# Layer 3's mean square taken from the layer norm's moments, and ScalarE for the last step of two quarters' norms

## The chip, the cores and the metric

The kernel runs on one core of one Trainium2 chip. The metric is device time in microseconds (us) of one execution; a kernel is run several times and the median counts. PE is the matrix engine (TensorE), DVE is VectorE, ACT is ScalarE, POOL is GpSimd and SP is the engine that issues most DMAs. [...]

## What is computed

The reference has four layers on an activation of 4 sequences of 1024 tokens with 128 features, in float32. Each layer is an attention-like mixer and a feed-forward block, each followed by a residual add and a layer norm without weights. Layer 2 has causal attention with 16 heads; the feed-forward blocks of layers 1, 2 and 3 route each token to some of 16, 8 and 32 experts. The change is in the mixer of layer 3:

```
def _layernorm(x, axis=-1, eps=1e-05):
    m = jnp.mean(x, axis=axis, keepdims=True)
    v = jnp.var(x, axis=axis, keepdims=True)
    return (x - m) / jnp.sqrt(v + eps)
...
    rms = jnp.linalg.norm(query, axis=-1, keepdims=True) * e ** (-0.5)
    x = query / (rms + EPS)
    u = jax.nn.silu(jnp.einsum('nbe,fe->nbf', x, u_w) + u_b)
    v = jax.nn.silu(jnp.einsum('nbe,fe->nbf', x, v_w) + v_b)
...
    y = _toeplitz_mix(vh, pos, zero, neg)
...
    out = u * y
    return jnp.einsum('nbf,ef->nbe', out, o_w) + o_b + query
```

`query` is the layer norm's result, with one row per token. Its root mean square `rms` can be had in two ways: from the normalised row itself, or from the norm's moments, since a row with variance v that was divided by sqrt(v + eps) has the mean square v / (v + eps).

## The kernel before, in words

**Tiles and parts.** The tokens lie in 32 tiles of 128 tokens by 128 features, in one SBUF tensor `x`. A quarter is 8 tiles: 256 positions of each of the 4 sequences. Layer 3 works on three parts: part a is quarters 0 and 1, part b is quarter 2, part c is quarter 3 (`self.first`, `self.rest`, L110).

**The norm.** `norm` (L185) takes a list of tiles. Per tile it issues `bn_stats` and `bn_aggr` on VectorE (L191, L192), which leave mean and variance in `mv`. Then it makes `rstd`, one over the root of variance plus epsilon, in one of several ways: with `by="act"` a Sqrt on ScalarE (L195) and a reciprocal on VectorE (L196); with `by="dve"` by `rsqrt` (L171), which is an integer guess and three Newton steps, 14 small VectorE operations. Last, one VectorE operation per tile subtracts the mean and multiplies by `rstd` (L205).

**Layer 3's mixer.** `l3_attn(part, exps)` (L1548) goes through the quarters of a part. `exps=True` is for part a, which runs while ScalarE computes the exponentials of layer 2's attention: Sqrt and Silu are avoided there, `by="dve"` is used, and Silu is put together from Tanh and VectorE operations. For a quarter the order is: norm (L1576); for each half of 4 tiles the squares (L1584), their sum per row (L1585), the root (by `rsqrt` at L1590 to L1592, or a Sqrt at L1594), scale and epsilon (L1595), the reciprocal (L1596), the row times this factor into `sq` (L1598), twice `x` plus a bias as the residual (L1600), and four PE transposes with a copy into `xq` (`transposes`, L159; the copy is L167 on ScalarE or L169 on VectorE). Then come the projections u and v with Silu (L1567, or L1570 to L1572), the Toeplitz mix on VectorE (L1626 to L1632), the output projection and residual (L1641), the second norm (L1643) and its transposes (`turned`, L1646).

**What follows it.** `l3_route` (L1650) makes router logits, softmax, the top 4 and, in `positions` (L1231), the place of each row in the lists of the experts (`pos...`, L1272). `spread` (L1309) scatters the rows into a list in DRAM with one indirect DMA on GpSimd per tile and choice (L1297). `l3_shared` (L1671) is the shared expert, whose result is added to `x` (L1687). `l3_experts` (through `small_experts`, L1699) gathers the list in groups of 4 tiles (L1328, issued by SP, which needs all scatters of the part) and works through it: transposes, gate and up, Silu (L1729), product (L1730), transposes, down, and a copy out (L1744 on ScalarE, L1747 on VectorE). `collect` (L1377) gathers each token's expert results with indirect DMAs on GpSimd and adds them to `x` (L1388); `finish` (L1782) and `close` (L1857) norm and store.

**What sets the order.** All of these are generators that issue instructions and then yield a planned cost in us: `yield (7.0,)` after the norm, `yield (4.0,)` after the mean square of a half, `yield (2.3,)` after a transposition, and so on. `mix(main, side, pace)` (L233) advances `side` until its planned cost times `pace` has caught up with what `main` has yielded; with `drain=False` the rest of `side` stays for later. `press` (L1844) advances the side alone until a condition holds. `abreast` (L1816) advances several generators at equal planned times. `served` (L1805) lets other generators go first as soon as their condition holds. An extra order is put on side instructions: each goes behind the latest instruction of the main on its engine (`queued`, L223).

In `all` (L1868), part a's mixer and routing are the side of layer 2's attention for the second half of the positions (`l2_attn(1)`, pace 1), then of layer 2's experts for the parts m and n, which also wait for their own routing; part b's mixer and routing are the side of part a's shared expert and experts (pace 0.75); then b's scatter, with part c's mixer and routing `abreast`, goes ahead of, and beside, part b's experts; part c's scatter and part b's collection go beside part c's experts; `close` of part c ends the kernel. After the last experts a branch on a flag can start a general path, which this data doesn't take.

Of the kernel before, what the change touches and what calls it, by code (L numbers as in the profile page):

```python
# [14 lines left out]
AF = mybir.ActivationFunctionType  # L15
ALU = mybir.AluOpType
AX = mybir.AxisListType
# [3 lines left out]
P = 128  # L21
B, L, D = 4, 1024, 128
# [8 lines left out]
QT = NT // NQT  # L31
# [43 lines left out]
class Kernel:  # L75
# [106 lines left out]
            ts(t, t, -0.5, 1.5, ALU.mult, ALU.add)  # L182
            tt(y, y, t, ALU.mult)

    def norm(self, tiles, by="act"):  # L185

        nc, n = self.nc, len(tiles)
        mv = self.tile(self.small, [P, n, 2], f"mv{n}")
        for t, x in enumerate(tiles):
            st = self.tile(self.small, [P, 6], "bn")  # L190
            nc.vector.bn_stats(st, x)  # L191
            nc.vector.bn_aggr(mv[:, t, :], st)  # L192
        rstd = self.tile(self.small, [P, n], f"rstd{n}")
        if by == "act":
            nc.scalar.activation(rstd, mv[:, :, 1], AF.Sqrt, bias=self.eps)  # L195
            nc.vector.reciprocal(rstd, rstd)  # L196
        else:
            ve = self.tile(self.small, [P, n], f"ve{n}")
            nc.vector.tensor_scalar(ve, mv[:, :, 1], LN_EPS, None, ALU.add)
            if by == "pool":  # L200
                nc.gpsimd.tensor_tensor(rstd, ve, self.mhalf[:, :n], ALU.pow)
            else:
                self.rsqrt(rstd, ve)
        for t, x in enumerate(tiles):
            nc.vector.tensor_scalar(x, x, mv[:, t, 0:1], rstd[:, t : t + 1], ALU.subtract, ALU.mult)  # L205

    def quarter(self, q):

# [1339 lines left out]
    def l3_attn(self, part, exps=False):  # L1548


        nc, tc, x, xT, col = self.nc, self.tc, self.x, self.xT, self.col
        stt = nc.vector.scalar_tensor_tensor
        NC = D13 // P
        with ExitStack() as ctx:
            cp = self.pool(ctx, "l3c" + part.name, right=True)
            vp = self.pool(ctx, "l3v" + part.name, right=True)
            ps = self.side
            wuv = self.load(cp, self.ins["l3_uv"])
            wo = self.load(cp, self.ins["l3_o"])
            if exps:  # L1560
                hb = self.tile(cp, [P, 2 * NC], "hb")
                nc.vector.tensor_scalar(hb, col["l3_b"], 0.5, None, ALU.mult)

            def silu(dst, pz, i):

                if not exps:
                    nc.scalar.activation(dst, pz, AF.Silu, bias=col["l3_b"][:, i : i + 1])  # L1567
                    return
                th = self.tile(vp, [P, BLK], "th", bufs=2)
                nc.scalar.activation(th, pz, AF.Tanh, bias=hb[:, i : i + 1], scale=0.5)  # L1570
                stt(dst, pz, col["l3_b"][:, i : i + 1], th, ALU.add, ALU.mult)
                stt(dst, pz, col["l3_b"][:, i : i + 1], dst, ALU.add, ALU.add)  # L1572

            for q in range(part.q0, part.q0 + part.nq):
                s = slice(q * QT, (q + 1) * QT)
                self.norm(self.quarter(q), by="dve" if exps else "act")  # L1576
                yield (7.0,)
                xq = self.tile(vp, [P, QC], "xq")
                rms = self.tile(self.small, [P, QT], "rms")
                for g in range(2):  # L1580
                    sg = slice(q * QT + g * 4, q * QT + g * 4 + 4)
                    r = rms[:, g * 4 : g * 4 + 4]
                    sq = self.tile(vp, [P, 4, D], "sq")
                    nc.vector.tensor_tensor(sq, x[:, sg, :], x[:, sg, :], ALU.mult)  # L1584
                    nc.vector.tensor_reduce(r, sq, AX.X, ALU.add)  # L1585
                    if exps:

                        ri = self.tile(self.small, [P, 4], "rmsi")
                        v = self.tile(self.small, [P, 4], "rmsv")
                        nc.vector.tensor_scalar(v, r, 1e-30, None, ALU.max)  # L1590
                        self.rsqrt(ri, v)
                        nc.vector.tensor_tensor(r, r, ri, ALU.mult)  # L1592
                    else:
                        nc.scalar.activation(r, r, AF.Sqrt)  # L1594
# [13 lines left out]
                    yield (2.3,)  # L1608
                u = self.tile(vp, [P, NC, B, TQ], "u")
                for c in range(NC):  # L1610
                    v = self.tile(vp, [P, B, TQ], "v")
                    for i, dst in ((1, v), (0, u[:, c])):
                        for g in range(2):
                            pz = self.tile(ps, [P, BLK], "s")
                            self.mm(pz, wuv[:, i, c * P : (c + 1) * P], xq[:, g * BLK : (g + 1) * BLK])
                            silu(dst[:, 2 * g : 2 * g + 2, :].rearrange("p b t -> p (b t)"), pz, i * NC + c)
                            yield (2.3,)

                    cf = col["toep"][:, c * 7 : (c + 1) * 7]
                    for i in range(B):  # L1620
                        y = self.tile(vp, [P, TQ], "y", bufs=1 if exps else 2)
                        for j in range(B):
                            lag = i - j
                            a = lag if lag >= 0 else 3 - lag
                            if j == 0:
                                nc.vector.tensor_scalar(y, v[:, j, :], cf[:, a : a + 1], None, ALU.mult)  # L1626
                            else:
                                stt(y, v[:, j, :], cf[:, a : a + 1], y, ALU.mult, ALU.add)
                        if exps:
                            stt(u[:, c, i, :], u[:, c, i, :], 0.25, y, ALU.mult, ALU.mult)  # L1630
                        else:
# [486 lines left out]
```

## Time and profile before

| | us |
|---|---|
| median of 3 runs | 2064.29 |
| lowest, highest of these | 2057.93, 2067.41 |
| the profiled execution, own time | 2440.36 |
| its span, first to last instruction | 2438.2 |
| PE busy | 1619.9 (66%) |
| VectorE busy | 1303.3 (53%) |
| ScalarE busy | 789.9 (32%) |
| GpSimd busy | 774.0 (32%) |
| mean granted TensorE clock | 0.813 |

The profile is of one execution, which took 18% more than the median of the unprofiled runs. Its times are counted from the first instruction. A row of the timeline names start, duration, engine, operation, output and inputs with their shapes, and in square brackets the engine's idle time before it with what released it ("remote" or "issue" where the profile shows no releaser). A row of a stretch has its limits, its length, then for each engine its busy time and its number of instructions, then the granted clock and the share of the DMA engines. Small operations overlap a little, so the pitch from start to start says more than a single duration.

### The profile page before, as it was taken

Reading aid. Unit: us, or ns where it says so; the run is one execution under the profiler, and the core shown is the slowest. Engines: PE = TensorE matmul, PEld = TensorE weight load, DVE = VectorE, ACT = ScalarE, POOL = GpSimd, SP = SyncE. Lnnn points to the kernel's source line nnn. Section 1 sums busy time; section 2 is a strip of 40 time slices with the busy share of each in tenths; the row PEclk is TensorE's granted clock in tenths of the full one; section 3 lists DMA queues with packets and bytes.
Section 4 is the critical chain, followed back from the end, with each engine's and each line's share of the span. In section 5 each row is a group of like instructions: output and inputs, shape, how many; then the busy total and the mean of one; then the engine's idle time right before and its main releaser. Section 6 shows DMA issues by size and latency. Waiting matters only on the chain. (4 is left out here: it accounts for less than half of the span.)

```text
span 2438.2 us, 27135 instructions
## 1 busy us (share of the span) xinstructions
PE 1619.9 (66%) x9017; PEld 962.6 (39%) x9017; DVE 1303.3 (53%) x3732; ACT 789.9 (32%) x1114; POOL 774.0 (32%) x701
## 2 busy tenths in 40 slices
PE   7535776875661775687968787887853898267080
PEld 3214333753320344545623232345532586154070
DVE  8767795655570564324535665464711378247053
ACT  5511372322230432222336454642211254122030
POOL 5531285145227002224132002002164201736704
PEclk9766787988785888888979898988876998577595
DMA  9930002334101014312120000031141141223132
GB/s 308 288 104 0 13 33 82 117 120 159 60 31 52 14 73 142 100 48 70 44 96 21 1 1 17 2 117 35 42 174 40 44 127 45 71 71 96 51 100 59
DMA packets 215530, 187.10 MB, mean 77 GB/s; under 512 B 16528, under 2 KB 194064, under 8 KB 214864
## 3 DMA queue, kind: packets, MB, share of 16 engines
q1 hardware_dynamic: 194672, 142.29, 18.5%
q0 software_dynamic: 20704, 42.86, 5.7%
q8 instruction: 84, 1.38, 0.2%
q14 instruction: 70, 0.57, 0.1%
HBM read 88.49 MB, written 96.60 MB: 76 GB/s over the span
## 5 line engine op out<-in xcount | busy, mean ns | idle before, releaser
L1051 ACT ACTIVATE pr<-sc 128x1024 f32<-128x1024 f32 x288 | 279.6, 1021 | 326.1 <-PE sc L157 197.7
L157 PE MATMUL gu<-ld,xgT 128*128 x640 | 172.1, 413 | 81.9 <-issue 36.6
L157 PE MATMUL sc<-qm,kT 32*128 32x512 f32 (+3 forms) x1536 | 200.2, 564 | 15.9 <-ACT pr L1051 12.0
L157 PE MATMUL s<-pr,va 128*32 128x512 f32 (+3 forms) x1536 | 177.3, 531 | 46.0 <-issue 27.9
L157 PEld LDWEIGHTS gu<-ld,xgT 128*128 128x128 f32 x640 | 123.6, 204 | 109.5 <-issue 48.0
L157 PE MATMUL gu<-wall,xgT 128*128 x304 | 161.0, 657 | 3.2 <-ACT xgT L167 2.0
L1057 DVE TENSOR_TENSOR pr<-pr,ld 128x512 f32<-128x512 f32 (+1 forms) x160 | 92.5, 581 | 101.3 <-ACT pr L1051 98.8
L169 DVE COPY hT<-tp 128x512 f32<-128x512 f32 x118 | 81.0, 686 | 120.7 <-PE tp L165 50.4
L165 PE MATMUL tp<-ld,hg 128*128 128x128 f32 x624 | 100.6, 285 | 50.4 <-DVE hT L169 35.4
L157 PEld LDWEIGHTS sc<-qm,kT 32*128 32x128 f32 x1536 | 85.5, 200 | 119.5 <-issue 66.6
L165 PE MATMUL tp<-ld,xg 128*128 128x128 f32 x396 | 66.3, 295 | 90.9 <-issue 50.7
L165 PEld LDWEIGHTS tp<-ld,hg 128*128 128x128 f32 x624 | 80.1, 147 | 104.8 <-DVE hT L169 42.2
L167 ACT COPY xgT<-tp 128x512 f32<-128x512 f32 x99 | 58.0, 587 | 195.4 <-PE tp L165 126.9
L1730 DVE TENSOR_TENSOR hg<-sg,gu 128x256 f32<-128x256 f32 x160 | 65.7, 416 | 102.5 <-ACT sg L1729 94.8
L1494 ACT ACTIVATE sg<-gu 128x512 f32<-128x512 f32 x76 | 45.2, 597 | 226.3 <-PE gu L157 115.3
L1297 POOL DMA_INDIRECT l1ra<-x,posl1a x64 | 95.6, 1494 | 60.5 <-DVE posl1a L1272 41.3
L1729 ACT ACTIVATE sg<-gu 128x256 f32<-128x256 f32 x160 | 60.6, 384 | 157.3 <-PE gu L157 85.7
L157 PE MATMUL pu<-xT,ld 128*128 128x512 f32 x104 | 65.0, 719 | 60.1 <-issue 58.5
L1297 POOL DMA_INDIRECT yt<-l1yr,posl1r x64 | 60.7, 948 | 139.2 <-DVE x L1388 78.8
L157 PEld LDWEIGHTS s<-pr,va 128*32 128x32 f32 x1536 | 38.7, 113 | 156.6 <-issue 110.6
L1496 DVE TENSOR_TENSOR hg<-sg,gu 128x512 f32<-128x512 f32 x76 | 51.8, 681 | 87.2 <-ACT sg L1494 43.9
L1297 POOL DMA_INDIRECT l1rr<-x,posl1r x64 | 61.7, 964 | 99.6 <-DVE posl1r L1272 80.4
(443 smaller groups left out, 3551.7 us busy)
## 6 DMA issues: line engine op xcount, KB each, us to landing
wall<-wall SPq DMA_DIRECT2D x16, 768.0 KB
l3ra<-zero SPq DMA_DIRECT2D x1, 6144.0 KB
ld<-in_l_w SPq DMA_DIRECT2D x2, 3072.0 KB
wall<-we SPq DMA_DIRECT2D x24, 256.0 KB
ld<-in_l_w SPq DMA_DIRECT2D x1, 6144.0 KB
l1ra<-zero SPq DMA_DIRECT2D x1, 5120.0 KB
l1rr<-zero SPq DMA_DIRECT2D x1, 5120.0 KB
xg<-l3ra SPq DMA_DIRECT2D x20, 256.0 KB
```

What stands on the lines that cost most here:

```text
L157: return self.nc.tensor.matmul(out, lhsT, rhs, start=start, stop=stop)
L165: nc.tensor.transpose(pt[:, k * P : (k + 1) * P], s, self.ident)
L167: nc.scalar.copy(dst, pt[:, : n * P])
L169: nc.vector.tensor_copy(dst, pt[:, : n * P])
L1051: nc.scalar.activation(pr, sc[h], AF.Exp)
L1057: nc.vector.tensor_tensor(d, d, cst["tril"].unsqueeze(1).unsqueeze(1).to_broadcast([P, 2, n, P]), ALU.mult)
L1297: ins = self.nc.gpsimd.indirect_dma_start(**kw)
L1494: nc.scalar.activation(sg, gu[:, 0, :], AF.Silu)
L1496: nc.vector.tensor_tensor(h, sg, gu[:, 1, :], ALU.mult)
L1729: nc.scalar.activation(sg, pg[:, :, 0, :], AF.Silu)
L1730: nc.vector.tensor_tensor(h[:, 2 * c : 2 * c + 2, :], sg, pg[:, :, 1, :], ALU.mult)
```

## The change

The norm gets an argument `on_act` and returns its moments and `rstd`. With `on_act`, minus mean times `rstd` is computed for all tiles in one VectorE operation (`off`), and the last step of each tile becomes a ScalarE activation, Identity of `rstd` times `x` plus `off`. In `l3_attn` both norms take it where `exps` is false, that is in quarters 2 and 3.

The mean square of all 8 tiles of a quarter comes from the variance in `mv`: its root times `rstd`, plus epsilon, inverted. The squares and their sums over 512 elements go, and the root is taken once for 8 columns in place of twice for 4. The planned costs become 6.0 after the first norm, 2.0 once for the root mean square, none for the halves' 4.0, and 5.0 after the second norm.

```diff
-    def norm(self, tiles, by="act"):
+    def norm(self, tiles, by="act", on_act=False):
...
+        if on_act:
+            off = self.tile(self.small, [P, n], f"off{n}")
+            nc.vector.scalar_tensor_tensor(off, mv[:, :, 0], -1.0, rstd, ALU.mult, ALU.mult)
         for t, x in enumerate(tiles):
-            nc.vector.tensor_scalar(x, x, mv[:, t, 0:1], rstd[:, t : t + 1], ALU.subtract, ALU.mult)
+            if on_act:
+                nc.scalar.activation(x, x, AF.Identity, bias=off[:, t : t + 1], scale=rstd[:, t : t + 1])
+            else:
+                nc.vector.tensor_scalar(x, x, mv[:, t, 0:1], rstd[:, t : t + 1], ALU.subtract, ALU.mult)
+        return mv, rstd
...
-                self.norm(self.quarter(q), by="dve" if exps else "act")
-                yield (7.0,)
+                mv, rstd = self.norm(self.quarter(q), by="dve" if exps else "act", on_act=not exps)
+                yield (6.0,)
...
+                if exps:
+
+                    v = self.tile(self.small, [P, QT], "rmsv")
+                    nc.vector.tensor_scalar(v, mv[:, :, 1], 1e-30, None, ALU.max)
+                    self.rsqrt(rms, v)
+                    nc.vector.tensor_tensor(rms, rms, mv[:, :, 1], ALU.mult)
+                else:
+                    nc.scalar.activation(rms, mv[:, :, 1], AF.Sqrt)
+                nc.vector.tensor_tensor(rms, rms, rstd, ALU.mult)
+                nc.vector.tensor_scalar(rms, rms, 1e-8, None, ALU.add)
+                nc.vector.reciprocal(rms, rms)
+                yield (2.0,)
                 for g in range(2):
...
-                    nc.vector.tensor_tensor(sq, x[:, sg, :], x[:, sg, :], ALU.mult)
-                    nc.vector.tensor_reduce(r, sq, AX.X, ALU.add)
-                    if exps:
...
-                        nc.vector.tensor_scalar(v, r, 1e-30, None, ALU.max)
-                        self.rsqrt(ri, v)
-                        nc.vector.tensor_tensor(r, r, ri, ALU.mult)
-                    else:
-                        nc.scalar.activation(r, r, AF.Sqrt)
-                    nc.vector.tensor_scalar(r, r, float(np.float32(D ** -0.5)), 1e-8, ALU.mult, ALU.add)
-                    nc.vector.reciprocal(r, r)
-                    yield (4.0,)
                     nc.vector.tensor_tensor(sq, x[:, sg, :], r.unsqueeze(2).to_broadcast([P, 4, D]), ALU.mult)
...
-                self.norm(self.quarter(q), by="dve" if exps else "act")
-                yield (6.0,)
+                self.norm(self.quarter(q), by="dve" if exps else "act", on_act=not exps)
+                yield (5.0,)
```

More of the change, by code (lines that the diff above doesn't have):

```diff
@@ L1574, in l3_attn @@
             for q in range(part.q0, part.q0 + part.nq):
-                s = slice(q * QT, (q + 1) * QT)
-                self.norm(self.quarter(q), by="dve" if exps else "act")
-                yield (7.0,)
+                mv, rstd = self.norm(self.quarter(q), by="dve" if exps else "act", on_act=not exps)
+                yield (6.0,)
                 xq = self.tile(vp, [P, QC], "xq")
                 rms = self.tile(self.small, [P, QT], "rms")
+                if exps:
[9 more added lines that the diff above has]
+                yield (2.0,)
                 for g in range(2):
                     sg = slice(q * QT + g * 4, q * QT + g * 4 + 4)
+                    sq = self.tile(vp, [P, 4, D], "sq")
                     r = rms[:, g * 4 : g * 4 + 4]
-                    sq = self.tile(vp, [P, 4, D], "sq")
-                    nc.vector.tensor_tensor(sq, x[:, sg, :], x[:, sg, :], ALU.mult)
-                    nc.vector.tensor_reduce(r, sq, AX.X, ALU.add)
-                    if exps:
-                        ri = self.tile(self.small, [P, 4], "rmsi")
-                        v = self.tile(self.small, [P, 4], "rmsv")
-                        nc.vector.tensor_scalar(v, r, 1e-30, None, ALU.max)
-                        self.rsqrt(ri, v)
-                        nc.vector.tensor_tensor(r, r, ri, ALU.mult)
-                    else:
-                        nc.scalar.activation(r, r, AF.Sqrt)
-                    nc.vector.tensor_scalar(r, r, float(np.float32(D ** -0.5)), 1e-8, ALU.mult, ALU.add)
-                    nc.vector.reciprocal(r, r)
-                    yield (4.0,)
                     nc.vector.tensor_tensor(sq, x[:, sg, :], r.unsqueeze(2).to_broadcast([P, 4, D]), ALU.mult)
```

## The prediction

> **What bounds the kernel now.** I read the page first, then busy time in stretches of the last third, then the timelines of ScalarE, VectorE and GpSimd there, then the waits around the edited lines. No engine is the bound as a whole: the page gives PE 66%, VectorE 53%, ScalarE 32%. The kernel is a chain of stages, each with another limit.
>
> ```profile
> 1248.00:1612.00 364.00, 310.21 (x2277) 112.56 (x2275) 209.80 (x647) 210.22 (x222) 27.96 (x29) 0.92 0.02 7
> 1973.00:1993.00 20.00, 16.69 (x106) 14.40 (x107) 15.41 (x37) 15.90 (x26) 0.00 (x0) 1.00 0.38 113
> 1993.00:2034.00 41.00, 40.48 (x255) 34.14 (x253) 30.59 (x76) 18.10 (x35) 0.00 (x0) 1.00 0.30 90
> 2034.00:2064.00 30.00, 24.75 (x90) 15.53 (x90) 24.08 (x122) 14.40 (x19) 0.00 (x0) 0.77 0.07 19
> 2270.00:2300.00 30.00, 0.00 (x0) 0.00 (x0) 0.00 (x0) 0.00 (x0) 22.68 (x25) 0.50 0.19 51
> ```
>
> Columns are the stretch, its length, then busy time of PE, weight loads, VectorE, ScalarE, GpSimd. The first row is the second half of layer 2's attention, beside which layer 3's attention runs for the first two quarters ("part a"): PE is busy 85%. Rows two to four are part a's experts with quarter 2's attention ("part b") beside them: PE is full at 1993 to 2034, but loses 3.3 us in the 20 us where b's norm and mean square run, and ScalarE is the fullest there after PE. From 2034 to 2064 nothing but the end of b's attention and its routing is left to wait for. The last row is a stretch where only GpSimd works.
>
> ```profile
> 1754.40 1.15 POOL L1297 DMA_INDIRECT l3ra<-x,posl3a  x1 [67.43 <-DVE posl3a L1272]
> ...
> 2064.11 0.99 POOL L1297 DMA_INDIRECT l3rb<-x,posl3b  x1 [119.14 <-DVE posl3b L1272]
> ...
> 2227.39 0.95 POOL L1297 DMA_INDIRECT yt<-l3ya,posl3a  x1 [0.30 <-issue]
> 2228.64 0.99 POOL L1297 DMA_INDIRECT l3rc<-x,posl3c  x1 [0.30 <-issue]
> ```
>
> GpSimd's timeline shows who starts each part's experts: the scatter of rows (64, 32 and 32 instructions, one per 1.265 us, so 81, 40 and 40 us) can't start before the positions, and the positions end the chain norm, attention, norm, routing. For a and b GpSimd waited for them; for c it did not: posl3c was written at 2224.35, and the scatter began when the gathers of part a's results ended.
>
> ```profile
> 1973.49 1.28 ACT L195 ACT_TABLE_LOAD   x1
> 1975.10 1.28 ACT L1729 ACT_TABLE_LOAD   x1
> 1977.55 1.28 ACT L1594 ACT_TABLE_LOAD   x1
> 1979.75 1.28 ACT L1729 ACT_TABLE_LOAD   x1 [0.49 <-PE gu L157]
> 1983.89 1.28 ACT L1594 ACT_TABLE_LOAD   x1
> 1985.41 1.28 ACT L1729 ACT_TABLE_LOAD   x1
> ```
>
> In b's window ScalarE changes tables six times, because each Sqrt falls between Silus of the experts.
>
> [...]
>
> ```profile
> L1430 ACT ACTIVATE am<-ld,em x24: 385/404/414, 521.7 to 605.1; 128x128 f32<-128x128 f32 x24
> L1584 DVE TENSOR_TENSOR sq<-x x8: 681/684/685, 1325.1 to 2086.9; 128x512 f32<-128x512 f32 x8
> L1585 DVE TENSOR_REDUCE rms<-sq x8: 679/686/687, 1325.8 to 2087.6; 128x4 f32<-128x512 f32 x8
> L1594 ACT ACTIVATE rms<-rms x4: 205/206/206, 1979.1 to 2088.3; 128x4 f32<-128x4 f32 x4
> ```
>
> L1430 also takes its scale from a column; three back to back started 0.30 us apart, so eight cost 0.40 + 7 x 0.30 = 2.5 us. Eight of VectorE's L205 take 2.14 us.
>
> **The change, part by part.**
>
> *Part a, mean square.* Each half quarter has L1584 at 1325.11 to the reciprocal's end at 1330.13: 5.0 us of VectorE, 10 a quarter. What replaces both halves is 19 small operations at a pitch of 0.20 us: 3.8. Saved: 6.2 us a quarter, 12 for two. PE is busy 85% there and VectorE 58%, so most of this is cover. PE issued 126 instructions in the 20 us where VectorE was at 82% (1320 to 1340), and 146 per 20 us where it was at 57% (1400 to 1440): even if VectorE made all of that difference, it is 2.7 us a quarter, and 6 of its 16 busy us go. I value both quarters at 1 us (0 to 4).
>
> *Part a, the planner.* A quarter cost 7 + 2 x 8.6 + 8 x 2.3 + 8 x 3 + 6 + 6 + 4.6 = 83.2 planned us; after, 6 + 2 + 2 x 4.6 + 18.4 + 24 + 6 + 5 + 4.6 = 75.2. Layer 2's second half offers 104 x 2.3 = 239 in the 366 us it takes (L1051, 1245.5 to 1611.4), 1.5 real us for each planned one. So the side is 16 planned us ahead at its end. Today the last norm of part a is left over: it runs at 1715 behind the routing of layer 2's last rows, and a's routing (1729 to 1754) falls beside the start of the last layer 2 experts. After, norm and two transposes (10 planned) move into the attention and the first half of the routing into the experts before. Then posl3a is ready about when those experts end, near 1741: 13 us sooner, and the 81 us scatter with it. What becomes late next is PE: the last layer 2 experts and the shared expert take some 61 + 42 us from 1733 in either kernel (20 tiles at the 3.05 us of the undisturbed ones at 1668, four blocks at 10.4). They only lose the routing as a competitor, 3 us (its matmuls on the mask held PE from 1741.5 to 1744.3). The experts of a start after the later of the two. I take 4 us (0 to 12).
>
> *Part b.* VectorE loses 2 x (0.68 + 0.69 + 0.17 + 0.18) = 3.4 and twice 2.14, and gains three small operations and two `off`, 1.0: 6.7 us less. ScalarE gains twice 2.5, loses one Sqrt (0.2), and since both Sqrts of the first norm read the same moments they can share a table: up to four loads, 5.1 us, go. In the window of 20 us PE lost 3.3; I expect 2 back (0 to 4). The norm's own latency doesn't shrink: 0.2 + 2.5 in place of 2.14 plus a handover, 0.5 to 1 us longer each time, and at the end of b's attention (2038.9, with the transposes and the copies L167 behind it on ScalarE) this is on the path: minus 1. If Identity did need a table of its own, each burst would cost two loads, 2.6 us; [...]. Behind the waiting ScalarE burst are Silus of the experts, for which PE waits: at most 2.5 us a burst, as VectorE's burst held the product hg before; taken as even.
>
> *Part b, the planner.* 8 x 0.75 = 6 planned us of expert work, 1.6 groups of 3.7; a group took 4.5 to 5.4 us here, so b's attention is 7 to 8 us ahead when a's experts end. Their end stays, since PE was full; the tail of 30 us to posl3b shrinks by what has moved ahead. I take 6 (2 to 10). GpSimd waited for posl3b, so the scatter of b, its experts and all behind move up.
>
> *Part c.* Its attention starts beside b's scatter, where VectorE waits for this scatter anyway:
>
> ```profile
> DVE x L1687 <- DMA l3rb<-x,posl3b: 28.8, 2, 16.1
> ```
>
> The residual add of the shared expert rewrites rows that the scatter reads. The second add went at 2106.48 and held all of VectorE's queue. The work saved lies mostly under this cover. posl3c comes sooner by 8 planned us, but GpSimd reaches the scatter of c only at 2228.6, behind the gathers of a, whose buffers are freed by adds that the planner places as before (the two branches run abreast, and the longer one, 144 against 128 planned us, is not changed). Gain 1 us (minus 5 to 8).
>
> The DMAs moved are the scatters; SP's queue keeps its order. Sum: 1 + 4 + 2 - 1 + 6 + 1 = 13 us. From the profiled execution, 2440.36 us (span 2438.2 and 2.2 around it), that is 2427. That execution is 18% above the median of 2064.29: it has stretches such as 2270 to 2300 with nothing but GpSimd's gathers. My terms are chain lengths in us, mostly outside of these, so I take the same 13 from the median: **2051**.
>
> **Rivals.**
>
> *Hidden.* PE sets the pace beside layer 2 and beside a's experts, so what leaves VectorE is free time, and what the planner moves ahead only fills PE elsewhere. For it: PE 40.48 of 41. Against it: 2034 to 2064 is exposed. Only the table loads and 2 us of tail count: about 4 us, 2060.
>
> *Slower: c gets behind the scatter.* Today half of c's normalised input (L1598 at 2072.25) is ahead of the two blocked adds L1687. With ScalarE's norm in between, its readers can be placed behind the second one. Then c's attention starts at 2106 in place of 2072, 34 us late less the 8 planned; posl3c at 2250, and the scatter of c, 22 us later than today, with nothing between it and the end to absorb it. 2064 - 10 + 22 = 2076. It decides from 4 us of slack (2224.35 to 2228.64) on, and outweighs the gains from about 14 us of delay. Against it: the norm of c was done by 2048, long before the block.
>
> *The saved steps don't move the route*, if the built program's own order outweighs the planned costs; the trace does show instructions out of written order (L1245 of b's routing at 2036.67, ahead of its norm's L205 at 2038.90). Then only 1 + 2 - 1 + 1 remain, 2061; it shares the case of "hidden".
>
> **How the numbers follow.** Forecast 0.47 (2040 to 2055 with the bounds of a and b), hidden 0.31 (2055 to 2064), slower 0.22 (2064 to 2080). A measurement of this kernel can tell about 0.5%, 10 us, from no change: the forecast lies just beyond it, and a part of its case is within. Faster 0.46, same 0.32, slower 0.22. The range that leaves 2 in 10 out is 2035 to 2074: the upper bounds of a and b together give 2064 - 29, and the slower case is held to its price less 2.
>
> **What would show it.** posl3a some 10 us earlier against the end of layer 2's second half; two table loads in b's window where there were six; 2034 to 2064 shorter by 5 or more; the scatter of c still right behind the gathers of a. It is wrong if posl3c trails those gathers, if b's stretch from a's last expert to posl3b keeps its 30 us, or if the layer 2 half grows by more than 3 us with the norm in it.

## The result, and the profile after

| | median, us | lowest to highest | runs |
|---|---|---|---|
| before | 2063.1 | 2057.93 to 2067.41 | 7 |
| after | 2045.37 | 2036.05 to 2049.51 | 7 |

The ratio is 0.992, with a 95% interval of 0.9896 to 0.9943: 17.7 us faster. The forecast was 2051.

Two chips took part, as far as the record tells, and on one of them both kernels take 18% longer; the profile of before that the prediction used came from there, the timed runs above from the other, so this section compares with a second profile of the kernel before (span 2063.2 us, its own time 2065.49) taken on the quicker one. The profile of after has a span of 2036.0 us. On the quicker chip single profiled runs lie up to some 7 us off the median of their kernel, in either direction, and their stages carry that.

First the busy time by stretches, the columns as above. The rows are the second half of layer 2's attention, then part a's experts where part b's norm and mean square run, the rest of these experts, and the stretch from a's last expert to b's positions. The kernel before:

```profile
1071.00:1412.00 341.00, 298.64 (x2286) 110.40 (x2282) 210.00 (x647) 210.86 (x223) 34.02 (x35) 0.94 0.03 9
...
1685.00:1705.00 20.00, 16.53 (x110) 14.47 (x109) 16.50 (x50) 15.46 (x26) 0.00 (x0) 1.00 0.47 139
1705.00:1749.00 44.00, 42.71 (x270) 35.87 (x268) 32.49 (x81) 20.31 (x40) 0.00 (x0) 1.00 0.29 88
1749.00:1777.00 28.00, 23.57 (x87) 15.17 (x88) 22.27 (x117) 13.32 (x17) 0.00 (x0) 0.76 0.06 15
```

The kernel after:

```profile
1070.00:1403.00 333.00, 293.40 (x2281) 109.86 (x2280) 209.29 (x626) 211.84 (x225) 33.14 (x33) 0.97 0.03 9
...
1665.00:1685.00 20.00, 17.80 (x107) 14.60 (x106) 11.30 (x27) 14.85 (x31) 0.00 (x0) 1.00 0.38 116
1685.00:1728.00 43.00, 39.17 (x257) 33.95 (x255) 36.00 (x106) 19.39 (x38) 0.00 (x0) 1.00 0.31 92
1728.00:1753.00 25.00, 20.23 (x61) 11.49 (x61) 14.97 (x74) 16.17 (x30) 0.00 (x0) 0.73 0.04 13
```

Layer 2's half is 8 us shorter, although VectorE is as busy in it as before (209.29 against 210.00): what was saved there was filled with part a's later steps. Most of the 8 us is not less waiting: PE's busy time fell by 5.2 (298.64 to 293.40, with five of its 2286 instructions fewer), the rest of the stretch, in which PE waits, by 2.8. The granted clock, the third number from the right, was 0.97 in place of 0.94. Within the half it falls to 0.50 in stretches of 3.4 to 10.2 us, which add up to 41 us in before and to 20.5 in after. At 0.50 a 32x512 score matmul took 1056 ns, at 1.00 588 (medians over the whole trace of after). In b's window VectorE fell from 16.50 to 11.30, PE's loss only from 3.5 to 2.2. The last stretch is 3 us shorter.

GpSimd's timeline of after, where each part's scatter begins:

```profile
1515.95 1.15 POOL L1305 DMA_INDIRECT l3ra<-x,posl3a  x1 [35.76 <-DVE posl3a L1280]
...
1754.40 0.99 POOL L1305 DMA_INDIRECT l3rb<-x,posl3b  x1 [109.52 <-issue]
...
1878.99 3.90 POOL L1305 DMA_INDIRECT yt<-l3ya,posl3a  x1 [0.30 <-issue]
1883.20 0.99 POOL L1305 DMA_INDIRECT l3rc<-x,posl3c  x1 [0.30 <-issue]
```

In the quick profile of before, a's scatter began at 1537.03 and b's at 1777.92: 21 and 23.5 us later than here. So nearly all is won by the start of a's scatter and kept from there on. The scatter of c still starts right behind the gathers of a's results; its positions had been written at 1862.5, 20.7 us earlier.

ScalarE in b's window:

```profile
1665.83 1.28 ACT L196 ACT_TABLE_LOAD   x1
1667.12 0.30 ACT L196 ACTIVATE rstd<-mv,eps 128x8 f32<-128x8 f32 x1
1667.33 0.19 ACT L1595 ACTIVATE rms<-mv 128x8 f32<-128x8 f32 x1
1667.54 1.28 ACT L1735 ACT_TABLE_LOAD   x1
1669.11 3.17 ACT L210 ACTIVATE x<-x,off,rstd 128x128 f32<-128x128 f32 x8
```

Two table loads where there were six. Both Sqrts share the first, and the eight Identities have none of their own: a Silu runs ahead of them at 1668.83 and one behind them at 1672.19, with no load in between. The prediction had assumed this; the trace of before shows it too, in the Identities of L406, one at 22.74 behind an Exp and one at 266.60 behind a Sigmoid, with no load in between. Eight took 3.17 us, where the prediction estimated 2.5.

The span by stages, each from the profile of one run (the three kernels in the middle are explained below):

| us | before | costs only | work only | no ScalarE | after |
|---|---|---|---|---|---|
| start to the half's first exponential | 1071.3 | 1068.4 | 1072.1 | 1071.4 | 1070.4 |
| to its last one | 340.3 | 351.0 | 333.6 | 334.2 | 332.6 |
| to posl3a | 125.0 | 112.6 | 125.3 | 112.4 | 112.5 |
| to the first load of a's list | 116.1 | 115.5 | 116.1 | 115.4 | 115.8 |
| to posl3b | 124.8 | 124.0 | 124.0 | 122.6 | 122.1 |
| to the end | 285.7 | 283.4 | 280.3 | 283.5 | 282.6 |

### The profile page after: what moved, and what is told of

It is laid out like the page before. It is cut to its first block, busy times and chain, and to the rows that moved or that the text cites. A ratio compares the mean times of both kernels' runs of the same rounds, so it can differ in the third digit from the quotient of the medians.

```text
span 2036.0 us, 27079 instructions
## 1 busy us (share of the span) xinstructions
PE 1542.5 (76%) x9017; PEld 933.2 (46%) x9017; DVE 1285.0 (63%) x3652; ACT 792.1 (39%) x1137; POOL 777.1 (38%) x701
## 5 line engine op out<-in xcount | busy, mean ns | idle before, releaser
L157 PE MATMUL sc<-qm,kT 32*128 32x512 f32 (+3 forms) x1536 | 189.5, 547 | 0.8 <-ACT pr L1059 0.8
L157 PE MATMUL gu<-ld,xgT 128*128 x640 | 164.0, 399 | 24.7 <-DVE hg L1736 15.2
L157 PE MATMUL s<-pr,va 128*32 128x512 f32 (+3 forms) x1536 | 160.3, 512 | 19.6 <-DVE x L997 7.3
L157 PE MATMUL gu<-wall,xgT 128*128 x304 | 147.9, 611 | 2.7 <-ACT xgT L167 2.0
L157 PEld LDWEIGHTS gu<-ld,xgT 128*128 128x128 f32 x640 | 119.4, 197 | 48.4 <-issue 18.0
L167 ACT COPY xgT<-tp 128x512 f32<-128x512 f32 x99 | 57.8, 585 | 138.1 <-PE tp L165 138.1
L165 PEld LDWEIGHTS tp<-ld,hg 128*128 128x128 f32 x624 | 78.2, 142 | 50.9 <-issue 32.4
L165 PE MATMUL tp<-ld,hg 128*128 128x128 f32 x624 | 97.0, 277 | 4.6 <-DVE hT L169 3.9
L165 PE MATMUL tp<-ld,xg 128*128 128x128 f32 x396 | 64.8, 291 | 44.0 <-DMA xg<-l3rc 13.6
L157 PE MATMUL yp<-ld,hT 128*128 x640 | 87.3, 280 | 3.5 <-DVE hT L169 2.0
L1305 POOL DMA_INDIRECT l2rm<-x,posl2m x16 | 15.9, 994 | 193.3 <-DVE posl2m L1280 188.7
L1305 POOL DMA_INDIRECT yt<-l1ya,posl1a x64 | 68.7, 1073 | 51.2 <-DMA l1ya<-yg 22.0
```

Source lines behind the costliest of these rows:

```text
L157: return self.nc.tensor.matmul(out, lhsT, rhs, start=start, stop=stop)
L165: nc.tensor.transpose(pt[:, k * P : (k + 1) * P], s, self.ident)
L167: nc.scalar.copy(dst, pt[:, : n * P])
L1305: ins = self.nc.gpsimd.indirect_dma_start(**kw)
```

## The experiments

### The planned costs and the work apart, and no ScalarE

Each result below is a median, with its ratio to the kernel before on the same chip and the 95% interval of this ratio. The kernel before once more, for the profile above:

> The kernel before, unchanged, for a second profile. The first one (2440 us) had stretches in which nothing but GpSimd worked and which the profile of the changed kernel (2036 us span) hardly has. Theory: those stretches belong to that one execution; this profile should lie near 2063 us, with stretches of that kind under 100 us in all. Rival: the kernel before has them in each profiled execution, and this one takes over 2300 us again.

One run took 2065.49 us, near 2063 as the theory had it; the median of before on this chip, over all its runs, was 2060.17.

Costs only, the kernel before with the planned costs of the change and all of its old work:

```diff
-                yield (7.0,)
+                yield (6.0,)
...
-                    yield (4.0,)
+                    yield (2.0 if g == 0 else 0.0,)
...
-                yield (6.0,)
+                yield (5.0,)
```

> The kernel before with nothing but the planned costs of the change (6.0 after the first norm, 2.0 and 0.0 after the two mean squares, 5.0 after the second norm): the same instructions, issued earlier beside the main work. Theory (order): most of the gain of 18 us is that the attention of layer 3 runs further ahead, so 8 to 14 us faster than before, some 2052. Rival (work): the gain is the VectorE and ScalarE work that left; then this is within 3 us of before, 2060 to 2066, or slower.

2060.53 us, ratio 1.0006 [0.9991, 1.0022].

Work only, the changed kernel with the old planned costs:

```diff
-                yield (6.0,)
+                yield (7.0,)
...
-                yield (2.0,)
+                yield (4.0,)
                 for g in range(2):
...
+                    if g:
+                        yield (4.0,)
...
-                yield (5.0,)
+                yield (6.0,)
```

> The changed kernel with the planned costs of before (7.0, 4.0 twice, 6.0): the work leaves, the place in the order doesn't. Theory (order): 3 to 7 us faster than before, 2056 to 2060. Rival (work): nearly the whole gain, 14 to 18 us, 2045 to 2049.

2057.9 us, ratio 0.9995 [0.9982, 1.0009].

No ScalarE, the changed kernel with the last step of all norms on VectorE:

```diff
-                mv, rstd = self.norm(self.quarter(q), by="dve" if exps else "act", on_act=not exps)
+                mv, rstd = self.norm(self.quarter(q), by="dve" if exps else "act", on_act=False)
...
-                self.norm(self.quarter(q), by="dve" if exps else "act", on_act=not exps)
+                self.norm(self.quarter(q), by="dve" if exps else "act", on_act=False)
```

> The changed kernel with every norm's last step on VectorE again (the mean square from the moments and the planned costs stay). Theory: the move to ScalarE is about even, since PE sets the pace beside part a's experts and the norm's latency grows by 0.5 to 1 us: within 3 us of the changed kernel, 2042 to 2048. Rival: VectorE was the limit near the end of part b's attention, and without the move 5 us or more are lost, 2050 or above.

2042.6 us, ratio 0.9928 [0.99, 0.9957], which can't be told from the whole change's 0.992. The move to ScalarE is worth nothing that was measured.

So this is the table of medians (new work with the new costs is the run without ScalarE; with the old costs it includes ScalarE's part):

| us | old planned costs | new planned costs |
|---|---|---|
| old work | 2060.2 | 2060.5 |
| new work | 2057.9 | 2042.6 |

Neither half alone moves the time by more than the noise; both together save 17.6. My theories had expected 8 to 14 us of costs only and 3 to 7 of work only. The stages show why. The new costs pull a's positions 12.5 us nearer to the end of layer 2's half, with either work. But with the old work the half itself grows by 10.7. Busy time in it, for costs only and for work only:

```profile
1068.00:1419.00 351.00, 299.35 (x2277) 111.19 (x2276) 220.36 (x668) 211.51 (x224) 34.22 (x35) 0.95 0.03 9
1072.00:1406.00 334.00, 294.58 (x2282) 109.45 (x2280) 198.59 (x605) 210.75 (x223) 33.86 (x34) 0.95 0.03 9
```

The length less PE's busy time is PE's waiting: 42.4 us in before, 51.7 in costs only, 39.4 in work only, 39.6 in after. With the old work the new costs add 9.3 us of it, with the new work 0.2. The waits of costs only, in the half (who waits on whom, total us, times, longest):

```profile
PEld s L165 <- issue: 18.7, 5, 10.8
PE s L165 <- DVE sq L1598: 9.9, 1, 9.9
```

and of the kernel before and of after in theirs:

```profile
PEld s L165 <- issue: 8.2, 5, 4.7
```

```profile
PEld s L165 <- issue: 9.5, 5, 4.8
...
PE s L165 <- DVE sq L1604: 4.0, 1, 4.0
```

L165 are the transposes of the scaled rows `sq`. The timeline of PE in costs only has the long wait at one place, the second half of the second quarter:

```profile
1291.85 1.09 PE L165 MATMUL s<-ld,sq 128*128 128x128 f32 x4 [9.95 <-DVE sq L1598]
```

VectorE's timeline says what stands ahead of `sq` there:

```profile
1278.42 0.69 DVE L989 TENSOR_TENSOR x<-s,x 128x512 f32<-128x512 f32 x1 [1.25 <-PE s L157]
...
1283.40 1.11 DVE L205 TENSOR_SCALAR x<-x,mv,rstd 128x128 f32<-128x128 f32 x4
...
1285.03 0.68 DVE L1584 TENSOR_TENSOR sq<-x 128x512 f32<-128x512 f32 x1
...
1291.01 0.69 DVE L1598 TENSOR_TENSOR sq<-x,rms 128x512 f32<-128x512 f32 x1
```

In VectorE's queue first comes layer 2's own residual (L989) and norm of a finished block, 6 us up to the end of L205, then the 6.7 us from the squares (L1584) to `sq`. In the profile of before such a norm ends at 1292.7 with the squares of the first half of that quarter behind it at 1292.60, but there the transposes come later in PE's queue, and PE finds other work until `sq` is there. The lower planned costs have moved the transposes of the second half forward to such a place.

PE stands with layer 2's scores queued behind the transposes: in these 9.95 us it starts no other matmul, and the next scores start at 1292.87, behind the transposes. ScalarE's exponentials then wait for the scores:

```profile
ACT pr L1051 <- PE sc L157: 136.7, 103, 22.7
```

126.2 us of that in before, 121.4 in after. The wait in costs only also leaves something behind: from 1286.9, within it, to 1297.2, over 5 us past its end, the granted clock was 0.50.

```profile
1288.00:1297.00 9.00, 5.15 (x21) 1.69 (x22) 4.54 (x18) 1.94 (x2) 0.00 (x0) 0.50 0.00 0
```

The four stretches at 0.50 in after begin behind 3.4 us, the length of the shortest of them, in which PE was busy for 18 to 42%; the seven in before that begin later than 5 us into the half, behind 52% at most. With a score matmul at 1056 ns in place of 588, a wait of PE can cost more than its length in these traces. Why after has fewer such stretches, and whether they make all of the 5.2 us of busy time, isn't shown.

With the new work the same placement leaves only layer 2's norm in the way, the factor for `sq` has been there for 12 us, and the wait is 4.0 us, not 9.9.

### From the positions to the experts

In all five kernels the first load of a's list follows posl3a by 115.4 to 116.1 us. The last copy of the results of layer 2's experts does not: it lies 61.7 us ahead of that load in before and 61.8 in work only, but 48.4, 48.7 and 49.1 in costs only, no ScalarE and after. So PE's side had some 13 us of slack, and the positions set the start. VectorE's timeline names the link. Before:

```profile
1628.05 0.35 DVE L1388 SCALAR_TENSOR_TENSOR x<-yt,wkl2m,x 128x128 f32<-128x128 f32 x1 [14.11 <-DMA yt<-l2ym,posl2m]
1630.51 0.61 DVE L1388 SCALAR_TENSOR_TENSOR x<-yt,wkl2m,x 128x128 f32<-128x128 f32 x2 [2.11 <-DMA yt<-l2ym,posl2m]
```

After:

```profile
1607.68 0.39 DVE L1396 SCALAR_TENSOR_TENSOR x<-yt,wkl2m,x 128x128 f32<-128x128 f32 x1 [2.47 <-DMA yt<-l2ym,posl2m]
1610.25 0.61 DVE L1396 SCALAR_TENSOR_TENSOR x<-yt,wkl2m,x 128x128 f32<-128x128 f32 x2 [2.18 <-DMA yt<-l2ym,posl2m]
```

These adds take layer 2's results of part m. Their gathers stand in GpSimd's queue behind the 64 scatters of part a. Before, and after:

```profile
1624.20 0.96 POOL L1297 DMA_INDIRECT l3ra<-x,posl3a  x1 [0.30 <-issue]
1625.46 0.98 POOL L1297 DMA_INDIRECT yt<-l2ym,posl2m  x1 [0.30 <-issue]
...
1603.94 0.95 POOL L1305 DMA_INDIRECT l3ra<-x,posl3a  x1 [0.30 <-issue]
1605.20 0.98 POOL L1305 DMA_INDIRECT yt<-l2ym,posl2m  x1 [0.30 <-issue]
```

The adds stand in VectorE's queue ahead of the products of a's shared expert, for which PE waits. PE's timeline, before:

```profile
1632.83 2.08 PE L157 MATMUL pu<-xT,ld 128*128 128x512 f32 x2 [16.17 <-DVE hs L736]
```

and after:

```profile
1612.57 2.08 PE L157 MATMUL pu<-xT,ld 128*128 128x512 f32 x2 [4.66 <-DVE hs L744]
```

The same wait is 3.72 us in costs only, 16.21 in work only and 4.13 in no ScalarE: it goes exactly with the planned costs, and what is left of it is all that a still earlier scatter could win there. This link is read from five traces of the quicker chip; no run changes it alone there.

### Part a alone, and VectorE's load put back

These two and all below ran on the slower chip, and are compared there: before took 2438.62 us beside these two and the first try with the gathers, 2441.3 beside the other four.

Part a alone, the change where `exps` is true and the code of before, planned costs too, where it is false (against the changed kernel):

```diff
+                new = exps
-                mv, rstd = self.norm(self.quarter(q), by="dve" if exps else "act", on_act=not exps)
-                yield (6.0,)
+                mv, rstd = self.norm(self.quarter(q), by="dve" if exps else "act", on_act=new and not exps)
+                yield (6.0 if new else 7.0,)
...
+                    if not new:
+                        nc.vector.tensor_tensor(sq, x[:, sg, :], x[:, sg, :], ALU.mult)
+                        nc.vector.tensor_reduce(r, sq, AX.X, ALU.add)
...
+                        yield (4.0,)
```

> The change for part a alone (mean square from the moments, its planned costs); parts b and c as before. The profiles put nearly all of the difference ahead of the start of part a's experts. Theory (part a): 13 to 17 us faster than before, 2043 to 2047. Rival (part b's tail of 6 us, as predicted): at most 10 us faster, 2050 or above.

2426.78 us, ratio 0.9952 [0.9932, 0.9971]. The whole change has 0.9932 [0.9907, 0.9958] on this chip (below): most of it is part a, and what b and c add isn't resolved.

The load put back: the changed kernel, with the squares, their sums and a second inverse root computed again on VectorE in part a's quarters, into tiles that nothing reads.

```diff
+                    idle = self.tile(self.small, [P, QT], "idle")
+                    for g in range(2):
+                        sg = slice(q * QT + g * 4, q * QT + g * 4 + 4)
+                        sqi = self.tile(vp, [P, 4, D], "sq")
+                        nc.vector.tensor_tensor(sqi, x[:, sg, :], x[:, sg, :], ALU.mult)
+                        nc.vector.tensor_reduce(idle[:, g * 4 : g * 4 + 4], sqi, AX.X, ALU.add)
+                    v2 = self.tile(self.small, [P, QT], "idlev")
+                    nc.vector.tensor_scalar(v2, idle, 1e-30, None, ALU.max)
+                    self.rsqrt(idle, v2)
```

> The changed kernel, with the squares, their sums and a second inverse root put back on VectorE in part a's quarters, into tiles that nothing reads: the load of before, without the waits of the normalised rows on it. Theory (load): VectorE's queue, in order, holds up layer 2's attention, so this loses what the planned costs alone lost: the second half of layer 2's attention 8 us longer than in the changed kernel, 2051 to 2058. Rival (latency): what counted was the wait of the transposes on the chain; then within 3 us of the changed kernel, 2042 to 2048.

2431.42 us, ratio 0.9962 [0.9938, 0.9985]. By the ratios that is 7 us slower than after, at the lower edge of the theory, but its interval and that of the whole change (0.9907 to 0.9958) overlap. Layer 2's half takes 360.3 us. Four traces on this chip with the changed kernel's instructions in the half (after, part a alone, the two gather runs of after) have 353.0 to 357.5, three with before's 365.6 to 365.9. The half in after, and with the load:

```profile
1246.30:1601.70 355.40, 305.38 (x2275) 111.42 (x2279) 209.25 (x626) 212.17 (x225) 30.08 (x31) 0.95 0.03 8
...
1251.20:1611.60 360.40, 307.39 (x2275) 111.91 (x2279) 215.40 (x664) 211.96 (x225) 27.81 (x28) 0.95 0.02 7
```

PE's waiting is 53.0 us with the load, 47.6 to 50.0 in those four, 53.8 to 57.3 in those three: the load brings back 3 to 5 us of it, while the wait on `sq` stays at 4.0. The split isn't clean. The load adds 6 us to VectorE's busy time in the half, where costs only has 11 more than after (220.36 against 209.29), with 38 and 42 instructions more; why it adds less isn't shown. And it stands in VectorE's queue ahead of the factor, so that the first half's `sq` is issued later too. So VectorE's load is a part of the price, and how large a part isn't shown.

### The same costs cut behind the transposes

If PE's wait at the transposes eats what costs only gains, the kernel before should gain when the same 8 planned us a quarter are cut behind the transposes:

```diff
                         else:
                             nc.vector.tensor_tensor(u[:, c, i, :], u[:, c, i, :], y, ALU.mult)
-                        yield (3.0,)
+                        yield (2.0,)
```

> The kernel before with all of its work, and with the same 8 planned us less per quarter, taken from the eight steps of the Toeplitz mix (3.0 each becomes 2.0), which lie behind the transposes, in place of the norm and the mean square ahead of them. Theory (the planned costs are worth 12 us of earlier routing, and with the old work they gain nothing only because PE then comes to the transposes of sq before the mean square is ready and stands there for 10 us): the half of layer 2 stays within 3 us of the kernel before, no wait of 9 us on sq, routing of part a 10 to 13 us earlier after it, and the time 8 to 12 us below the kernel before (ratio 0.994 to 0.996). Rival (whatever is pulled into the half of layer 2 costs there what it saves later, unless work is taken away): the half is some 10 us longer, and the time as before (0.999 to 1.002).

2432.65 us, ratio 0.9976 [0.9959, 0.9993]: between the two. posl3a comes 127.8 us after the half, 14.7 sooner than in before's profile (142.5), and the half is 371.7, 5.8 longer. The net of 8.9 is close to the measured 8.6, but 7.8 of it are gone at the first load of a's list (192.2 us after posl3a, where before has 184.4) and 5.6 come back up to posl3b, so the agreement may be chance. My theory was that no long wait on `sq` would come up; it does, only shorter:

```profile
PE s L165 <- DVE sq L1598: 6.9, 1, 6.9
```

VectorE's timeline shows why:

```profile
1458.70 0.18 DVE L1596 RECIPROCAL rms<-rms 128x4 f32<-128x4 f32 x1
...
1460.70 0.69 DVE L989 TENSOR_TENSOR x<-s,x 128x512 f32<-128x512 f32 x1 [1.25 <-PE s L157]
...
1465.68 1.11 DVE L205 TENSOR_SCALAR x<-x,mv,rstd 128x128 f32<-128x128 f32 x4
1466.71 0.68 DVE L1598 TENSOR_TENSOR sq<-x,rms 128x512 f32<-128x512 f32 x1
```

The factor is ready here (L1596), and layer 2's norm alone lies between it and `sq`. So it takes no saved work to gain from the planner, the wait is again about as long as the growth of the half (6.9 and 5.8; 9.9 and 10.7 in costs only, on the other chip), and what makes it is the meeting with layer 2's norm, which the mean square then makes longer or not.

The changed kernel beside it, as the reference on this chip:

> The changed kernel once more, as the reference for the three others on this chip. Its ratio to the kernel before is 0.992 if the chip is like the first one, 0.992 to 0.996 if it is one of those on which both take some 2430 us.

2425.09 us, ratio 0.9932 [0.9907, 0.9958].

### The gathers ahead of the scatter

If the gathers behind the scatter are the link, then gathers ahead of it should win in the kernel before and not in after. The first try put `rows_in(m2)` ahead of what was left of the side:

```diff
-                    on = self.chain(on, self.rows_in(m2))
+                    on = self.chain(self.rows_in(m2), on, iter([(0.0,)]))
```

> The kernel before, with the 16 gathers of part m's layer 2 rows put ahead of part a's scatter on GpSimd. In the kernel before VectorE waited 16 us for these gathers, which are queued behind the 81 us scatter, and with it PE in the shared expert. Theory (gathers behind the scatter were the link by which a's routing set the time): the gathers fill GpSimd's idle time before posl3a, the wait goes, 8 to 14 us faster than before, 2046 to 2052. Rival (the scatter itself was the link): part a's experts still start some 2 to 5 us after the last scatter, and the gain is as the scatter moves: none, or slower where the gathers delay it.

2452.66 us, ratio 1.0061 [1.0039, 1.0083]; and in the changed kernel:

> The changed kernel with the same exchange. Its VectorE waits only 5 us for the gathers, and posl3a comes right after the rows to gather are there, so the gathers delay the scatter by up to 17 us. Theory: PE's own work then sets the start of part a's experts; 0 to 5 us faster than the changed kernel, 2040 to 2045. Rival: the scatter, now later, sets it, and 5 us or more are lost, 2050 or above.

2439.31 us, ratio 1.0005 [0.9984, 1.0027]. The exchange was not the one that I meant. `press` had already issued four scatters, and the gathers, behind them in GpSimd's queue, stood through the wait of 67.40 us for posl3a too: the first began at 1762.23. GpSimd in the first of the two:

```profile
1756.92 1.16 POOL L1297 DMA_INDIRECT l3ra<-x,posl3a  x1 [67.40 <-DVE posl3a L1272]
...
1760.91 1.02 POOL L1297 DMA_INDIRECT l3ra<-x,posl3a  x1 [0.31 <-issue]
1762.23 0.98 POOL L1297 DMA_INDIRECT yt<-l2ym,posl2m  x1 [0.30 <-issue]
```

They pushed the scatter's end 20 us back. The kernel before lost 14 us by it, the changed one some 18 (from a ratio of 0.9932, below, to 1.0005): a later end of a's scatter does cost time.

The second try takes the scatter out of `onward` and issues it behind the gathers:

```diff
-                self.chain(self.rows_in(a2), self.onward(a, True)),
+                self.chain(self.rows_in(a2), self.routed3(a)),
...
-                    on = self.chain(on, self.rows_in(m2))
+                    on = self.chain(on, self.rows_in(m2), self.spread("l3", a, K3), iter([(0.0,)]))
```

(`routed3` is `onward` without its last line.)

> The kernel before with the gathers of layer 2's results for part m on GpSimd ahead of the whole scatter of part a, not behind it. Theory (part a's experts start late because VectorE stands 16 us on those gathers, which stand behind the scatter): the gathers fill the 20 us in which GpSimd waits for posl3a, the wait of 14 to 16 us at the adds goes, a's experts start 8 to 16 us earlier against posl3a, and the time is 6 to 14 us below the kernel before (ratio 0.993 to 0.997). Rival (PE's own path sets the start of a's experts): 0 to 3 us, ratio 0.998 to 1.001.

2440.13 us, ratio 0.9996 [0.9979, 1.0014].

> The same order in the changed kernel. Theory: its VectorE waits only 2.5 us at those adds, and posl3a is there at about the time at which part m's results are written, so the gathers now delay the scatter by up to 20 us and take that from its end: between 3 us faster and 10 us slower than the changed kernel. Rival (the gathers bind in both kernels alike): 8 to 14 us faster than the changed kernel.

2440.62 us, ratio 0.9995 [0.997, 1.002]; 15.5 us slower than after.

In the kernel before, the gathers now ran while GpSimd waited for the positions, a's list was loaded 172.2 us after posl3a where it had been 184.6, and posl3b came 22.8 us earlier than in before's profile. The time didn't follow: the first result of b's experts was only 6.7 us earlier, and the end 4.2. In the traces of this chip engines stop for tens of us while GpSimd issues indirect DMAs, up to 47.6 us in the first profile of before, often with no releaser in the profile, and such a stop of 28.79 us lies in between. ScalarE's timeline in b's shared expert:

```profile
2099.78 0.60 ACT L735 ACTIVATE sg<-pg 128x512 f32<-128x512 f32 x1 [7.79 <-PE s L157]
2129.16 0.58 ACT L167 COPY xq<-s 128x512 f32<-128x512 f32 x1 [28.79 <-remote]
```

Nor did the wait of 14.11 us exist on this chip, in before's profile, in that form: a stop of 30 us in layer 2's last experts covered it. So the run doesn't test the link where I had seen it, on the quicker chip, and there the order wasn't tried. In the changed kernel the scatter began 19 us after posl3a, and the time went up by 15.5, more than the 10 that I had allowed (its profiled run took 2458.75 us, 18 over its median). So the gathers' place behind the scatter isn't what binds there.

On this chip the changed kernel gains 16 us all the same (2441.3 to 2425.09), without the wait of 14 us that it takes away on the other one. So this link isn't the only way in which earlier positions can become time, and what it is here stays open.

## Why the prediction was right, and where its steps were not

*The sum* was 13 us and 17.7 came. The direction was right, and a's positions came earlier as said; that the sum came so near is in part luck, since several of its terms were off, in both directions.

*Part a, mean square, 1 us (0 to 4).* With the old planned costs it is worth about that: 2.3 us between the medians, with an interval of the ratio that holds 1. With the new ones it is worth 17.9, parts b and c included. In the half, costs only and after differ by 18.4 us: 12.1 of PE's waiting, the wait on `sq` 5.9 of it, and 6 of PE's busy time. The step that failed is that the two were valued as separate terms. I had asked what of VectorE's work lies beside PE's, and not what else would be in VectorE's queue ahead of `sq` once part a's steps were placed elsewhere. And I priced PE's waiting alone, not what the clock of 0.50 behind a wait costs. The sign named for it, "if the layer 2 half grows by more than 3 us with the norm in it", comes up in costs only, and not in the change.

*Part a, the planner, 4 us (0 to 12).* "13 us sooner" for posl3a was right, counted from the end of layer 2's half: 12.5. (The scatter of 81 us is 64 pitches; with the stops in it, it took 88.9 in the profile that I read, and 88 to 90 wherever nothing else lies in between.) The rule "the experts of a start after the later of the two" was too, but I took PE as the later one. PE had 13 us of waiting in it that the trace of before shows on the quicker chip, 16.17 us in a's shared expert, and that wait ended with gathers which stood behind the scatter. I read the scatter's end as the only thing that follows from posl3a, and didn't follow GpSimd's queue one entry further, to the gathers of part m and who waits for them. By the stages all of the 12.5 arrived at a's experts, so the term was mis-sized by 8.5. The profile that I read was of the slower chip, where the stops hide this wait. That it is the link is read from the traces and not tested.

*Part b, the window, 2 us (0 to 4).* PE's loss in 20 us fell by 1.3. The table loads went from six to two, as said.

*The norm's latency on ScalarE, minus 1.* Eight Identities took 3.17 us. In the second norm a table load stood ahead of the eighth (1.28 us at 1730.73), as before one stood ahead of the copy L167 there. Taking ScalarE out again changed neither the time (0.9928 against 0.992) nor the stretch to posl3b (122.6 and 122.1 us): the move, with what it takes off VectorE, is worth about zero.

*Part b, the planner, 6 us (2 to 10).* The stretch from a's last expert to posl3b shrank by 3, not by 5 or more, and all from a's first load to posl3b by 2.7. I assumed that PE was full among a's experts and that what moves ahead costs nothing there. In after it is not full: 39.17 of 43 us, where it was 42.71 of 44, while VectorE rose from 32.49 to 36.00. VectorE got b's later steps earlier, and PE's losses there ate half of the lead. That last sentence is read from these rows, and no run isolates it.

*Part c, 1 us.* From posl3b to the end 285.7 became 282.6, and the scatter of c stands right behind the gathers of a. The waits of the residual adds on the scatter of b are a little shorter than before's 28.7 us on this chip, not gone:

```profile
DVE x L1693 <- DMA l3rb<-x,posl3b: 25.9, 2, 13.6
```

*The rivals.* "Hidden" (2060) would hold for either half of the change alone, and not for both. "c gets behind the scatter" fell: posl3c leads its scatter by 20.7 us. "The saved steps don't move the route" fell with the 12.5 us, which came with either work.

*What stays open.* The stages of the single profiles add up to more than the medians give, by 6 to 10 us in each of the four kernels compared with before; before's own profiled run was 5 us over its median, and the other four lie 1 to 7 us below theirs. Of the shorter layer 2 half, VectorE's load, the earlier rows and the clock aren't separated beyond what stands above. And the link by the gathers wasn't tested on the chip whose traces show it.

## What to carry to other kernels

When instructions are placed by planned costs, a cut in the cost and a cut in the work belong together: the lower cost moves readers and producers to other places in the queues of two engines, and here it paid in full only where nothing long of another stage then stood ahead of the producer (ratio 1.0006 for the costs alone, 0.9928 with the work, without ScalarE's part). Test the two apart, and look for a new wait of the engine that sets the pace. Compare this engine's busy time too, not only its waits: here most of what the half lost was busy time (5.2 of 8 us), at a higher granted clock (0.97 in place of 0.94). When a stage moves ahead, follow the queue of each engine that it uses past its own last instruction: here the traces of one chip point to the next user of GpSimd's queue, four steps from the change, as what turned earlier positions into time.

## What the runs showed of the hardware that was not expected

The same kernel took 2060 us on one chip and 2440 on another, with the same instructions, and this change had the same direction on both (0.992 and 0.9932). In the trace of the quicker one there are 11 stretches of over 3 us in which neither TensorE, VectorE nor ScalarE works, 80 us together and 11.4 at most. In the slower one there are 31, 270 us together and up to 47.6, and 28 of them lie where GpSimd issues indirect DMAs. GpSimd itself keeps its pitch of 1.26 us on both. The cause of these stops stays open; they are half of the difference, and for 23 of the 31 the trace shows no releaser, the longest among them.
